# A four-layer graph network on one core: a queue of its own for layer 1's last row chain, and later checks in layer 2's wide pass

## The chip, the cores and the metric

The kernel runs on one core of one Trainium2 chip. The metric is the device time of one execution in microseconds (us). Three runs of the kernel before the change took 1104.93, 1107.02 and 1113.25 us; their median is 1107.02 us.

The engines are called as the profile calls them: PE multiplies matrices (PEld loads its stationary operand), DVE is the vector engine, ACT the scalar engine, POOL is GpSimd, and SP issues the large DMA loads.

## The reference, cut to what matters

`x` has 4096 rows of 64 numbers, `adj` is a 4096 x 4096 matrix of zeros and ones in float32 (64 MB). Four layers follow each other, each of the form `x = layernorm(x + f(x, adj))`:

```
# layer 0: mean over neighbours, a linear map, relu, rows of unit length
deg = sum(adj, 1) + 1
z = concat([x, (adj @ x + x) / deg]) @ W + b ; out = relu(z) / norm
# layer 1: hyperbolic attention, curvature c = 1/r**2
adj_att = sigmoid(left[:, None] + right[None, :] + b) * adj
support = einsum('ij,ijd->id', adj_att, logmap(x_i, x_j))
out = proj(expmap(x, support))
# layer 2: of each row's edges the last 100 count, with weights halving from the end
w = mask * where(pos > 0, 0.5 ** (k - pos), 0) ; out = w @ (x @ weight) + bias
# layer 3: as layer 1, with curvature 1
```

The fast path holds only if every entry of `adj` is 0 or 1. So each loaded piece of `adj` is also checked, once in the whole program: a vector instruction counts the entries that are neither. Any such entry would send the program into a slow path, which is not run here.

## The kernel before, in words

The columns of `adj` are cut into four groups `s` of 1024 output rows, taken as 3, 2, 1, 0 (`GROUPS`). In each layer a group walks over 16 loads `g` = 15 down to 0 (`load`, L698: 1 MB each, one tile `edges`, six buffers), each of two blocks `j` = 2g+1 and 2g of 128 source rows. So `adj` is read four times, 256 loads in all. A buffer is free for the load six later when PE, and the check if there is one, have read it.

Layer 0 has on PE eight matmuls for a load (L1414). Layers 1 and 3 (`attend`) have for each block the logits and squares on PE (L1059 to L1065), a sigmoid and a square on ACT (L1074, L1077), and two instructions on DVE (L1080, L1082), whose result goes back to PE (L1037). Layer 2 has a wide pass over groups 3 and 2 together (`wide_pass`), then a narrow pass for group 1 and one for group 0. In a pass, PE counts edges into a running PSUM tile (`count`, L1569), ACT takes a power of two of it (`weights_of`, L1576), and PE adds up with the rows of `halves` (`add_up`, L1581). The next block's count goes into the same PSUM tile, so PE waits there for ACT's reading. `halves` of group s is made by `supports(s)`, from the group's finished rows of layer 1: ACT casts to `x_hl` (L1252), POOL takes the remainder (L1253), PE transposes (L1258), ACT copies to `x_t` (L1261), PE multiplies (L1268), ACT and DVE write `halves` (L1274, L1275).

Between these stand the row chains: `end_0` after a group of layer 0, `move` after a group of layers 1 and 3, `end_2` after a group of layer 2, each with some hundred small instructions one after the other. They are Python generators in two queues. A call of `tick(1)` (one for each block and one for each pair of blocks in `attend`, four for each load in layer 0, two for each block in the wide pass) lets the head of each queue emit its instructions up to its next `yield n`; then it rests n ticks. Only the head of a queue moves. The wide pass has no ticks in its first five blocks. `need(tag)` ticks until a piece is done: in the wide pass it is asked for group 1 before load g = 7 (`need((2, 1))`) and for group 0 before g = 3 (`need((2, 0))`). What `need` emits stands in the instruction stream with none of the pass's own work between.

`move(1, 1)` is queued (`later(move_s)`, queue 0) when `attend` of group 1 ends, and runs on POOL with a few DVE instructions, beside group 0's attention. `move(1, 0)`, the last, is queued behind it in queue 0 and runs on DVE (its names end in `_1`). `supports(1)` waits in queue 1 for the tag of `move(1, 1)`; `supports(0)` is queued in queue 0 behind `move(1, 0)`. Both `move`s keep their 64 columns `u` and the row sums in one tile `u_1` with one buffer.

Inside `tc.manual_schedule(engines=FIXED)`, which holds layers 0 and 2, PE and ACT execute in the order of the program text; DVE and POOL are put in order by the framework's planner at build time.

`check` (L838, one DVE instruction on 1 MB and a small one that reads its count): layer 0 checks the loads with even g, layer 2 those with odd g, for all groups. Layer 0 writes its unused output into `junk`, layer 2 into the tile `t` of the attention.

Of the kernel before, what the change touches and what calls it, by code (L numbers as in the profile page):

```python
# [10 lines left out]
F32 = mybir.dt.float32  # L11
# [8 lines left out]
P = 128  # L20
N = 4096
D = 64
# [8 lines left out]
NW = N // WW  # L31
WB = WW // P
# [26 lines left out]
def gnn_stack_kernel(  # L59
# [15 lines left out]
    nc = tc.nc  # L75
    V = nc.vector
# [11 lines left out]
    for src, at in ((b0, 0), (b2, D), (b_att1, 2 * D), (b_att3, 2 * D + 1), (r1, 2 * D + 2)):  # L88
        n = src.shape[0]
# [479 lines left out]
    def stream(fits):  # L569

        with ExitStack() as st:

            def pool(name, bufs=1, **kw):
                return st.enter_context(tc.tile_pool(name=name, bufs=bufs, **kw))
# [4 lines left out]
            row = pool("f_row")  # L579
            lefts = pool("f_lefts", 2)  # L580
            aux = pool("f_aux", 1, space=PSUM)
            GROUPS = tuple(reversed(range(NW)))
# [5 lines left out]

            FIXED = {mybir.EngineType.PE, mybir.EngineType.Activation}
            ROW_ENGINES = FIXED | {mybir.EngineType.DVE}  # L590
            queues, place, done, held = ([], []), [0, 0], set(), []

# [32 lines left out]
                    mark(True)  # L627

            def later(steps, second=False, wait=0):
                queues[second].append([steps, place[1] + wait])  # L630

            def in_turn(tag, *parts):
                for part in parts:
                    yield from (part or ())
                done.add(tag)
# [4 lines left out]

            def need(tag):
                while tag not in done:
                    assert queues[0] or queues[1], tag
                    tick(1)

            def soon():
# [49 lines left out]
            def load(s, g):  # L696
                a = loads.tile([P, 2, WW], F32, name="edges")
                nc.sync.dma_start(a, adj[s, :, 2 * g : 2 * g + 2, :])  # L698

                return a, a.rearrange("p b i -> p (b i)").bitcast(BF16)[:, 1::2]  # L700

            def grp(name, bufs=None):
                kw = {"bufs": bufs} if bufs else {}
                return row.tile([P, WB, D], F32, name=name, **kw)

            def nums(name, n=WB):
                return row.tile([P, n], F32, name=name)
# [81 lines left out]
            for h in range(2):  # L789
                of = slice(h * D, (h + 1) * D)  # L790
# [11 lines left out]
            for k in range(3):  # L802
                part = float(np.float16(rest))
# [294 lines left out]
            def move(layer, s, sums, curve):  # L1098
# [8 lines left out]
                last = s == GROUPS[-1]  # L1107
                G = Small(not last, "_1" if last else "")
                E = V if last else nc.gpsimd
                nums = G.nums  # L1110
                k, d, uu = nums("k"), nums("d"), nums("uu")
                w, sq = (grp("y"), grp("xw")) if last else (grp("w_att"), grp("sq"))

                if last and layer == 3:

                    all_u = ys.rearrange("p k f -> p (k f)").bitcast(F32)[:, : WB * (D + 1)]
                    all_u = all_u.rearrange("p (k f) -> p k f", f=D + 1)
                else:
                    all_u = row.tile([P, WB, D + 1], F32, name="u_1")
                u, sum_1 = all_u[:, :, :D], all_u[:, :, D]  # L1120
                for part in range(2):
                    yield from free()
                    t = take(F32, P, 2, 2, D + 1)
                    for i in range(2):
                        cols = slice((2 * part + i) * P, (2 * part + i + 1) * P)
                        nc.tensor.matmul(t[:, i], sums[:, cols], centre, start=True, stop=True)
                    yield near()
                    nc.scalar.copy(  # L1128
                        all_u.rearrange("p (h k) f -> p k h f", h=2)[:, 2 * part : 2 * part + 2], t
                    )  # L1130
                    held.pop()
                    yield near()
                E.tensor_mul(w, xg, u)  # L1133
# [34 lines left out]
                y2, xy, den, p, q = (nums(n) for n in ("y2", "xy", "den", "p", "q"))  # L1168
# [18 lines left out]
                px, qd, w2, t = nums("px"), nums("qd"), nums("w2"), nums("mt")  # L1187
# [11 lines left out]
                n = yield from G.rsqrt(t, "n", 12)  # L1199
# [103 lines left out]
            with ExitStack() as lp:  # L1303
# [94 lines left out]
                with tc.manual_schedule(engines=FIXED):  # L1398
                    for s in GROUPS:
                        sums = [ps.tile([P, W], F32, name="acc") for _ in range(2)]  # L1400
                        counts = [ps.tile([P, W], F32, name="acc") for _ in range(2)]
                        parts = ((first, sums, P), (third, counts, D + 1))
                        for g in reversed(range(NB // 2)):
                            a, edge = load(s, g)
                            if s == GROUPS[0] and 2 * g % WB == WB - 2 and g > WB // 2:
                                parts_of(2 * g // WB - 1)
                            if g % 2 == 0:
                                check(s, g, a, own.tile([P, 2, WW], BF16, name="junk"))
                            for k in (1, 0):
                                j = 2 * g + k  # L1410
                                for lhs, accs, m in parts:
                                    for h in range(2):
                                        at = k * WW + h * W
                                        nc.tensor.matmul(  # L1414
                                            accs[h][:m], lhs[:, j, :], edge[:, at : at + W],
                                            start=j == BLOCKS[0], stop=j == BLOCKS[-1],
                                        )
                            if g == s * WB // 2 + 1:

                                for lhs, accs, m in parts:  # L1420
                                    for h in range(2):
                                        for k in range(SB):
                                            nc.tensor.matmul(
                                                accs[h][:m, k * P : (k + 1) * P],
                                                lhs[:, s * WB + h * SB + k, :], ident_b,
                                                start=False, stop=False,
                                            )
                            if s == GROUPS[0] and g == NB // 2 - 3:
                                curve1, curve3, att1, att3 = constants()
                                nc.scalar.dma_start(w2_sb, w2)  # L1430
                                nc.scalar.dma_start(w2_twice[:D], w2)
                                nc.scalar.dma_start(w2_twice[D:], w2)
                                later(in_turn((0, s), linear(0, s, w0_sb[:D, :], own_part)))
                            tick(4)
                        need((0, s))
                        tops = []
                        for h in range(2):
                            top = sb.tile([P, W], F32, name="top")
                            nc.scalar.copy(top, sums[h])
                            low = sb.tile([D + 1, W], F32, name="low")  # L1440
                            nc.scalar.copy(low, counts[h][: D + 1])
                            tops.append((top, low))
                        later(end_0(s, tops))
                        if s > 0:
                            own_of = linear(0, s - 1, w0_sb[:D, :], own_part)
                            later(in_turn((0, s - 1), own_of))
# [11 lines left out]
            def attention(layer, curve, rates, behind):  # L1458

                need((layer, GROUPS[0]))  # L1460
                for n, s in enumerate(GROUPS):
                    if n:
                        need((layer, s, "left"))
                    anchored[0] = n > 0
                    then = GROUPS[n + 1] if n + 1 < NW else None
                    sums = attend(layer, s, rates[n], then)
                    move_s = in_turn((layer, s, "moved"), move(layer, s, sums, curve))
                    if n:
                        later(
                            in_turn((layer + 1, s + 1), there((layer, s + 1, "moved")), behind(s + 1)),  # L1470
                            True, 9,
                        )
                    later(move_s)
                    if n + 1 == NW:
                        later(in_turn((layer + 1, s), behind(s)))
                anchored[0] = False


# [78 lines left out]

            def load_2(s, g):
                a, edge = load(s, g)
                if g % 2 == 1:  # L1560
                    junk = sb.tile([P, 2, WW], F32, name="t", bufs=3).bitcast(BF16)
                    check(s, g, a, junk[:, 0, :].rearrange("p (b i) -> p b i", b=2))
                return edge
# [64 lines left out]
            t, g = nums("m1", 1), nums("g1", 1)  # L1628
# [26 lines left out]
    with tc.tile_pool(name="fit_ps", bufs=1, space=PSUM) as ps:  # L1655
        t = ps.tile([1, P], F32, name="fit_t")
# [52 lines left out]
```

## Time and profile before

| what | value |
|---|---|
| median of three runs | 1107.02 us |
| profiled execution: span from first to last instruction | 1106.6 us (the profile gives no other time of it) |
| PE, DVE, ACT, POOL busy | 1001.9, 915.5, 803.1, 273.1 us |
| mean granted clock of PE | 0.966 |
| one check (L838) | 2.29 us, 64 of them |
| layer 0, about | 0 to 190 us |
| layer 1, about | 190 to 522 us |
| layer 2: wide pass, two narrow passes, about | 515 to 625, 625 to 761 us |
| layer 3, about | 761 to 1106 us |

The stages are read off the lines of the chain of waits (L1414, L1037, L1569 and L1581, L1037 again). A line of the chain is: start, duration, engine, tile written, source line, number of instructions. A line of a timeline has besides the operation, its operands and, in brackets, the idle time of the engine before it and what ended that.

### The profile page before, as it was taken

The numbers are of one execution on the slowest core, as the hardware profiler recorded it, in microseconds if no ns is written. First come the engines' busy times: TensorE is split into PE (matmuls) and PEld (weight loads), VectorE is DVE, ScalarE is ACT, GpSimd is POOL, SyncE is SP. The second block draws the span as 40 slices with busy tenths as digits, with TensorE's granted clock in tenths as the row PEclk, the third lists the DMA queues.
The fourth block names the chain that finished last, engine by engine and source line by source line (L and its number), as shares of the span: only waits on it lengthen the run. The fifth ranks groups of instructions, "written<-read, shape, count | busy, mean of one in ns | idle before, by whom it ended". The sixth has DMA issues, their size and how long they took to land.

```text
span 1106.6 us, 13832 instructions
## 1 busy us (share of the span) xinstructions
PE 1001.9 (91%) x4949; PEld 392.4 (35%) x4949; DVE 915.5 (83%) x1452; ACT 803.1 (73%) x892; POOL 273.1 (25%) x649
## 2 busy tenths in 40 slices
PE   4998998889999999998998998789899999999980
PEld 2454554333333333332333332223333333333320
DVE  5777977989999999999456484545999999999996
ACT  0003123879999999897676788889899998998960
POOL 0011212010144443525500010000001444346173
PEclk8999999889999999999998999799999999999995
DMA  9999999536565565654877987477545656666400
GB/s 341 378 419 380 370 423 396 190 131 244 191 240 219 188 238 219 228 194 148 333 304 275 362 289 261 155 270 285 203 169 211 251 214 229 228 227 227 164 1 23
DMA packets 38581, 271.63 MB, mean 245 GB/s; under 512 B 4710, under 2 KB 4710, under 8 KB 5734
## 3 DMA queue, kind: packets, MB, share of 16 engines
q1 hardware_dynamic: 37728, 270.03, 64.8%
q8 instruction: 41, 0.67, 0.2%
q10 hardware_dynamic: 774, 0.63, 0.2%
q14 instruction: 38, 0.31, 0.1%
HBM read 269.58 MB, written 1.05 MB: 245 GB/s over the span
## 4 chain that ended last, share of the span: by engine, by line
PE 55%; DVE 24%; ACT 9%; DMA 5%; POOL 3%; issue 2%; ACTq 0%; SPq 0%; POOLq 0%; DVEq 0%
PE acc L1037 15%; PE z L1569 9%; DVE t L1082 7%; PE z L1059 7%; PE z L1065 6%; PE z L1062 6%; DVE t L1080 6%; DMA edges<-in_adj_dram 4%; PE acc L1581 3%; PE acc L1414 3%; ACT sq L1077 3%; ACT sq L1576 2%; DVE junk L838 2%; ACT sig L1074 1%; PE z L1581 1%
## 5 line engine op out<-in xcount | busy, mean ns | idle before, releaser
L1080 DVE SCALAR_TENSOR_TENSOR t<-z,sig 128x1024 f32<-128x1024 f32 x256 | 308.8, 1217 | 13.0 <-ACT sq L1077 6.8
L1077 ACT ACTIVATE sq<-z,turn 128x1024 f32<-128x1024 f32 x256 | 277.8, 1111 | 45.1 <-PE z L1065 18.4
L1082 DVE SCALAR_TENSOR_TENSOR t<-sq,t 128x2048 f32<-128x2048 f32 x128 | 297.3, 2322 | 0.5
L1074 ACT ACTIVATE sig<-left_b,right 128x1024 f32<-128x1024 f32 x256 | 285.9, 1146 | 1.9 <-DVE t L1080 1.3
L1037 PE MATMUL acc<-t,xe 128*64 128x512 f32 x1024 | 255.2, 608 | 17.2 <-DVE t L1082 16.8
L1059 PE MATMUL z<-edges,two_i 128*128 128x512 bf16 x512 | 201.2, 393 | 7.4 <-DVE t L1080 7.4
L1065 PE MATMUL z<-dst,src 74*128 74x512 f16 x512 | 195.5, 382 | 0.0
L1062 PE MATMUL z<-lo_hi,hi_lo 128*128 128x512 f16 x512 | 194.4, 380 | 0.0
L1576 ACT ACTIVATE sq<-z,at_edge 128x512 bf16<-128x512 f32 (+1 forms) x192 | 149.3, 828 | 46.0 <-PE z L1569 43.5
L838 DVE SCALAR_TENSOR_TENSOR t<-edges 128x2048 bf16<-128x2048 f32 x32 | 73.0, 2287 | 54.2 <-DMA edges<-in_adj_dram 54.2
L1037 PEld LDWEIGHTS acc<-t,xe 128*64 128x64 f32 x1024 | 63.8, 136 | 145.6 <-issue 83.8
L1569 PE MATMUL z<-edges,pass_by 128*128 128x512 bf16 x248 | 89.5, 401 | 17.9 <-ACT sq L1576 17.8
L1414 PE MATMUL acc<-edges,first 128*128 128x512 bf16 x256 | 80.1, 394 | 17.6 <-DMA edges<-in_adj_dram 17.3
L1059 PEld LDWEIGHTS <-two_i 128*128 128x128 bf16 x512 | 50.3, 98 | 128.9 <-issue 82.3
L1569 PE MATMUL z<-edges,enter 128*128 128x512 bf16 x256 | 91.0, 398 | 0.0
L1414 PE MATMUL acc<-edges,third 128*65 128x512 bf16 x256 | 80.0, 394 | 0.0
L838 DVE SCALAR_TENSOR_TENSOR junk<-edges 128x2048 bf16<-128x2048 f32 x32 | 73.1, 2286 | 4.7 <-DMA edges<-in_adj_dram 4.4
L1065 PEld LDWEIGHTS <-src 74*128 74x128 f16 x512 | 49.2, 96 | 70.5 <-issue 8.0
L1062 PEld LDWEIGHTS <-hi_lo 128*128 128x128 f16 x512 | 50.4, 98 | 57.1 <-issue 11.7
L1581 PE MATMUL acc<-sq,halves 128*64 128x512 bf16 x384 | 62.5, 403 | 1.0 <-ACT sums L1088 0.8
L869 POOL TENSOR_TENSOR sq<-z 128x512 f32<-128x512 f32 x8 | 14.2, 1776 | 164.3 <-DVE z L868 132.2
L1133 POOL TENSOR_TENSOR w_att<-x,u 128x512 f32<-128x512 f32 x6 | 15.6, 2595 | 141.2 <-ACT u L1128 141.2
(375 smaller groups left out, 940.9 us busy)
## 6 DMA issues: line engine op xcount, KB each, us to landing
edges<-in_adj_dram SPq DMA_DIRECT2D x256, 1024.0 KB, 4.7
x<-in_x_dram SPq DMA_DIRECT2D x4, 256.0 KB
out_dram<-x ACTq DMA_DIRECT2D x2, 256.0 KB
out_dram<-x SPq DMA_DIRECT2D x2, 256.0 KB
w_sb<-in_L_gnn_W_dram ACTq DMA_DIRECT2D x1, 32.0 KB, 4.8
w_twice<-in_L_gnn_weight_dram ACTq DMA_DIRECT2D x2, 16.0 KB, 8.6
given<-in_L_gnn_b_dram ACTq DMA_DIRECT2D x1, 0.2 KB
given<-in_L_gnn_bias_dram ACTq DMA_DIRECT2D x1, 0.2 KB
```

The source lines that it names most:

```text
L838: V.scalar_tensor_tensor(junk, a, 0.0, a, ALU.not_equal, ALU.not_equal, accum_out=odd[:, n : n + 1])
L1037: it = nc.tensor.matmul(acc[h * D : (h + 1) * D, :], xe[:, j, :], t[:, k, h * W : (h + 1) * W], start=j == BLOCKS[0], stop=j == BLOCKS[-1],)
L1059: nc.tensor.matmul(half, two_i, edge[:, at : at + W], start=True, stop=False)
L1062: nc.tensor.matmul(half, hi_lo[:, of], lo_hi[:, to], start=False, stop=False)
L1065: last = nc.tensor.matmul(half, src[:, of], dst[:, to], start=False, stop=True)
L1074: nc.scalar.activation(sig, left_b, AF.Sigmoid, bias=right[:, j : j + 1])
L1077: nc.scalar.activation(sq[:, k], zp, AF.Square, bias=turn, scale=-1.0 / UNIT)
L1080: V.scalar_tensor_tensor(t[:, k], zp, 0.0, sig, ALU.max, ALU.mult)
L1082: V.scalar_tensor_tensor(t, sq, HIGH**2, t, ALU.add, ALU.mult)
L1414: nc.tensor.matmul(accs[h][:m], lhs[:, j, :], edge[:, at : at + W], start=j == BLOCKS[0], stop=j == BLOCKS[-1],)
L1569: nc.tensor.matmul(z[:, h : h + W], lhs, rhs[:, h : h + W], start=j == BLOCKS[0], stop=True, skip_group_check=True,)
L1576: nc.scalar.activation(w, z[:, :n], AF.Exp, bias=at_edge, scale=-LN2)
```

## The change

It has two parts.

First, a third queue. For the last group of layer 1, `move(1, 0)` and `supports(0)` go to queue 2; each tick then steps `move(1, 1)` in queue 0, `supports(1)` in queue 1 and the head of queue 2. The last `move` of layer 1 takes its `u` from the tile `z0` and its row sums from a small tile of their own; the row sums are copied there by DVE (two small copies), and ACT copies 256 columns instead of 260.

Second, which checks are made when. For groups 3 and 2 (those of the wide pass), layer 2 checks g = 0, 1, 2, 3, 5, 7, 9, 11 where it checked 1, 3, ..., 15; layer 0 checks g = 4, 6, 8, 10, 12, 13, 14, 15 where it checked 0, 2, ..., 14. The number of checks stays 64. Groups 1 and 0 stay as they were.

```diff
-            queues, place, done, held = ([], []), [0, 0], set(), []
+            queues, place, done, held = ([], [], []), [0, 0], set(), []
...
             def later(steps, second=False, wait=0):
-                queues[second].append([steps, place[1] + wait])
+                queues[int(second)].append([steps, place[1] + wait])
...
+            def checked_later(s, g):
+
+                return g in (0, 1, 2, 3, 5, 7, 9, 11) if s in GROUPS[:2] else g % 2 == 1
...
                 else:
-                    all_u = row.tile([P, WB, D + 1], F32, name="u_1")
-                u, sum_1 = all_u[:, :, :D], all_u[:, :, D]
+                    all_u = None if last else row.tile([P, WB, D + 1], F32, name="u_1")
+                if all_u is None:
+                    u, sum_1 = grp("z0"), nums("sum_1")
+                else:
+                    u, sum_1 = all_u[:, :, :D], all_u[:, :, D]
...
-                    nc.scalar.copy(
-                        all_u.rearrange("p (h k) f -> p k h f", h=2)[:, 2 * part : 2 * part + 2], t
-                    )
+                    of = slice(2 * part, 2 * part + 2)
+                    if all_u is None:
+                        nc.scalar.copy(
+                            u.rearrange("p (h k) f -> p k h f", h=2)[:, of], t[:, :, :, :D]
+                        )
+                        V.tensor_copy(
+                            sum_1.rearrange("p (h k) -> p k h", h=2)[:, of], t[:, :, :, D]
+                        )
+                    else:
+                        nc.scalar.copy(
+                            all_u.rearrange("p (h k) f -> p k h f", h=2)[:, of], t
+                        )
...
-                            if g % 2 == 0:
+                            if not checked_later(s, g):
                                 check(s, g, a, own.tile([P, 2, WW], BF16, name="junk"))
...
-                    later(move_s)
+                    apart = 2 if n + 1 == NW and layer == 1 else 0
+                    later(move_s, apart)
                     if n + 1 == NW:
-                        later(in_turn((layer + 1, s), behind(s)))
+                        later(in_turn((layer + 1, s), behind(s)), apart)
...
             def load_2(s, g):
                 a, edge = load(s, g)
-                if g % 2 == 1:
+                if checked_later(s, g):
```

More of the change, by code (lines that the diff above doesn't have):

```diff
@@ L642, in need @@
                 while tag not in done:
-                    assert queues[0] or queues[1], tag
+                    assert any(queues), tag
                     tick(1)
```

## The prediction

> **What bounds the kernel now.** I read the page first, for the span and the engines.
>
> ```profile
> span 1106.6 us, 13832 instructions
> PE 1001.9 (91%) x4949; PEld 392.4 (35%) x4949; DVE 915.5 (83%) x1452; ACT 803.1 (73%) x892; POOL 273.1 (25%) x649
> ```
>
> PE is busy 91% of the span, so a gain has to come from the remaining 9%, and from its slow-clock stretches. Second, the chain of waits between 500 and 680 us, where the change acts.
>
> ```profile
> 565.02 2.12 ACT sq L1576 x2
> 567.14 0.51 ACT x_hl L1252
> 567.72 1.17 POOL x_hl L1253
> 568.93 0.64 PE aux L1258 x8
> 569.59 1.02 ACT x_t L1261
> 570.65 0.64 PE z L1268 x16
> ...
> 594.69 0.52 ACT x_hl L1252
> 595.28 1.68 POOL x_hl L1253
> 597.00 0.63 PE aux L1258 x8
> 597.66 1.02 ACT x_t L1261
> 598.73 1.03 PE z L1268 x16
> 599.76 3.41 PE z L1569 x8
> ```
>
> These are two holes in the wide pass. At each, `need` stops the pass until `supports` has run from ACT to POOL to PE to ACT to PE. The first is for group 1, the second for group 0. ACT's timeline sizes them: L1576 starts for a new block every 2.90 us, but at 565.02 and, two blocks later, at 575.13: 10.11 - 5.80 = 4.3 us lost. The second: 592.58 to 605.87, so 13.29 - 5.80 = 7.5 us lost. Together 11.8.
>
> Third, DVE's timeline at the border of layers 1 and 2.
>
> ```profile
> 517.95 2.28 DVE L838 SCALAR_TENSOR_TENSOR t<-edges 128x2048 bf16<-128x2048 f32 x1
> ...
> 520.16 2.28 DVE L1082 SCALAR_TENSOR_TENSOR t<-sq,t 128x2048 f32<-128x2048 f32 x1
> ...
> 529.00 0.16 DVE L754 TENSOR_SCALAR n<-mt 128x8 int32<-128x8 int32 x1
> ```
>
> A check of the wide pass stands ahead of the last product of layer 1, which PE (0.97 us) and ACT (2.15 us) then wait for. Three more follow at 522.36, 524.57 and 526.78, and `move(1, 1)`, ready on POOL at 513.52, gets its L754 only behind them.
>
> Fourth, layer 0, where half of the checks lie: SP's waits, then DVE and PE near the start.
>
> ```profile
> SPq L698 <- DVE junk L838: 101.0, 28, 6.8
> ```
>
> ```profile
> 18.04 2.27 DVE L838 SCALAR_TENSOR_TENSOR junk<-edges 128x2048 bf16<-128x2048 f32 x1
> ...
> 22.57 0.29 DVE L1332 COPY given_b<-aux 128x131 f32<-128x131 f32 x1
> ```
>
> ```profile
> 22.91 1.01 PE L822 MATMUL aux<-one_row,att_row 1*128 1x1 f32 x4 [4.34 <-DVE given_b L1332]
> ```
>
> In layer 0 the loads wait 101.0 us (28 times, 6.8 the longest) for checks to release a buffer, and 37.2 for PE's L1414. The DMA engines are busy 96 to 99% there (windows from 20 to 195 us), so a load issued late is mostly not caught up. At the start PE waits 4.34 us for `given_b`, behind the checks at 18.04 and 20.35.
>
> **The third queue.** I counted ticks from the yields. The pass's first tick is in block 26. In the kernel before, `move(1, 1)` ends in the first tick of `need((2, 1))`, the 23rd. Only then does `move(1, 0)` begin; its first product starts at 566.74, its rows are written at 591.5, 24.8 us later, and by its last rest of 13 ticks it ends in the first tick of `need((2, 0))`. So `supports(0)` is emitted there, all of it.
>
> After, `move(1, 0)` steps from the first tick: its copies in blocks 26 and 25, its tanh in the 11th tick (block 21), the rest in the 12th, its end in the 25th, which lies inside `need((2, 1))`. `supports(1)` keeps its place, ticks 23 to 29. So `supports(0)` starts inside the first hole, ends in the next block, and the second hole is gone: -7.5 us. What takes its place:
> - *The first hole grows.* One `x_hl` buffer serves both groups, and ACT is in order: the second cast (0.55 with its gap) stands ahead of `x_t` of group 1. Then eight transposes (0.64) before PE counts again, and after that count the product of group 0 (0.64, and about 0.1 for its copy). Together +1.9.
> - *Work that lay in the hole.* The eight matmuls with `centre` ran at 566.74 to 567.9 while PE waited. They move into full blocks: +1.2. ACT has 0.78 idle per block: the `u` copies (0.39, 0.38) fit; the square (0.63) and a `halves` cast (0.58) may cost 0.3. DVE's two new copies (0.2 each, by its 128x8 rows) lie in its idle time (16.6 of 40 us busy from 525 to 565); without cover they cost 0.4.
> - *The slow clock.* After the second hole PE ran slow: 1.05 us a pair of matmuls at 599.57, 0.61 at 604.69; L1569 and L1581 take 4.4 us where they take 2.4. PE had idled 2.64 and 1.10 us. In the first hole it idled 1.03 and 1.08 and stayed fast. Without `centre` it idles from 566.8 to 568.9 and then some 1.6, 3.7 us in all, as in the second hole. So a drop may move there: +2.0, or nothing. I take 6 in 10 of it, 1.2.
>
> [...]
>
> Sum: -7.5 + 1.9 + 1.2 + 0.3 + 1.2 = -2.9, between -4.4 (no drop, all on ACT hidden) and +2 (a drop, and ACT waiting 4 us once for DVE). Queued behind such waits: tanh holds all later L1576, hence PE. By rows, DVE needs from the last copy to the tanh 1.1 + 1.3 + 4.1 = 6.5 us (568.35 to 576.68, less a `halves` product and a wait), and seven ticks of half a block leave 10.1; a check in front takes 2.29. The rest takes 10 us, 14.6 with two checks (576.82 to 591.44), and has five blocks, 14.5, up to the hole. POOL's side of `move(1, 1)` gets DVE's L754 some 9 us earlier and is not late.
>
> **The checks in layer 2.** g = 15 and 13, four checks, leave the border. The last L1082 can start at 518.03 instead of 520.16. PE still counts until 521.5, so PE gains about 1.0 and ACT up to 2.1: -1.5, between -1.0 and -2.1. The four checks come back at g = 2 and 0, where DVE is busy 7.6 of 25 us (600 to 625) and PE, not DVE, releases the buffers (SP waits 217.9 us for L1569 there and later, 5.6 for these checks). I cost them at nothing; without that cover they are 4 x 2.29 = 9.2.
>
> **The checks in layer 0.** Two places get two more, and each group's last two go, where they delay no load that starves.
> - *Group 3, from 0 us.* The check of g = 15 can run before 17.66, as DVE idles 6.40 us there behind a small DMA; that of g = 13 likely lands before `given_b`: +2.3 on PE's first wait, and on the tenth load (30.20), as DMA has drained by 32.7. If DVE's order puts two checks into the idle stretch, nothing; if it puts four behind 17.66, +4.6. It can also free a place (-2.3). I take +1.0.
> - *Group 2, from 55 us.* g = 15 lands at 54.9, in DVE's 3.87 us wait for PE: free. g = 13 falls into `end_0`'s chain, which has 1.16 us idle there: +1.1 to +2.3 on the check at 80.96, which releases the loads at 83.23, 89.76 and 93.12. I take +1.7.
>
> Sum for layer 0: +2.7, from -2.3 to +6.9. From there everything is serial, so shifts add: -2.9 - 1.5 + 2.7 = -1.7. Against the profiled execution that is 1106.6 - 1.7 = 1104.9. The median of the runs stands 0.4 above the span, so **1105.3**.
>
> **Rivals.**
> - *Layer 0 eats it all (slower).* Checks at g = 13 to 15 hold buffers while DVE works on constants and rows: +6.9 instead of +2.7, 1109.5. For it: 101.0 us of waiting on checks. Against it: DVE's idle 6.40 and 3.87 us. It decides from +4.4 on.
> - *The rows come too early (slower).* Ahead of the tanh or of `x(0)` in the hole DVE runs two checks (4.6), ACT stands, PE stands behind it, and the clock drops: 4.6 + 4.6 less slack, about +9, 1114. For it: no slack on PE per block. Against it: the counted 10.1 and 14.5 us.
> - *More goes than one hole (faster).* At 689.12, 696.87 and 701.91 ACT takes three early sigmoids of layer 3 in the narrow pass, each with two table loads: 1.28 + 1.15 + 1.28 = 3.7, 11.1 in all. The order that is planned anew may leave some out. With two out, layer 0 at nothing and no clock drop: 1105.3 - 7.4 - 2.7 - 1.2 = 1094. Against it: nothing in the diff touches them.
> - *Nothing moves.* If `move(1, 0)` ends later than the hole, the stop moves behind it: 1107.
>
> **How the numbers follow.** Forecast 0.50 (its own range 1101 to 1110), layer 0 0.18, early rows 0.12, more than one hole 0.12, nothing moves 0.08. About 1% (11 us) is what a measurement of this kernel can tell from no change: the runs spread over 8 us. Below 1096: most of the third rival, 0.11, the rest of it lying just above. Above 1118: half of the second and a tail of the first with the 6 us that the slowest run stands above the median, 0.11. Within 1%: 0.78. The range 1094 to 1116 takes in -2.1 - 4.4 - 2.3 with one early sigmoid gone (1107.0 - 8.8 - 3.7 = 1094.5) and the second rival with 2 us on top.
>
> **What would show it.** Right: no `need` stop near 590, L1576 at 2.90 us through there, first hole about 2 us longer or slow afterwards, the last L1082 of layer 1 without a check ahead of it, layer 0 ending 1 to 5 us later with more waiting on L838. Wrong: tanh (L1164) waiting over 1 us, PE waiting for `x_hl` over 5 us, a changed number of table loads, or layer 0 as early as before.

## The result, and the profile after

The changed kernel takes 1107.76 us (median of 14 runs, 1105.63 to 1114.76); the kernel before, run beside it on the same chip, takes 1107.74 us (14 runs, 1102.04 to 1115.95). The ratio is 1.0001, 95% interval 0.9984 to 1.0019: no difference to within 0.2%, where the prediction had 1105.3 us.

The profiled execution of the changed kernel took 1114.76 us and is the slowest of its 14. In it PE also ran slow (granted clock 0.50) from 671.8 to 678.6 and from 729.8 to 736.7 us, where the blocks of the narrow passes took some 4 us longer than before; in the profile before, a slow stretch begins at 672.6 us, but is only 3.4 us long, and from 710.2 to 765 us the granted clock is 1.00. So below, places are compared and not spans. First the page.

```profile
span 1113.0 us, 13744 instructions
PE 1004.0 (90%) x4862; PEld 394.4 (35%) x4949; DVE 915.9 (82%) x1454; ACT 804.6 (72%) x892; POOL 272.8 (25%) x649
```

Busy times are those of before within 2.1 us on each engine. Nothing was saved or added in work, so whatever changed is in waits and in the clock. The lines answer to those of before with numbers higher by 4 (early in the file) to 17 (L1569 is now L1586, L1576 is L1593).

**The wide pass.** ACT's timeline of the changed kernel where the first hole was (start, duration, instruction, and in brackets ACT's idle time ahead of it and what ended that):

```profile
563.31 2.12 ACT L1593 ACTIVATE sq<-z,at_edge 128x1024 bf16<-128x1024 f32 x2 [0.78 <-PE z L1586]
565.32 0.62 ACT L1268 CAST x_hl<-x 128x512 f16<-128x512 f32 x1
568.85 0.62 ACT L1268 CAST x_hl<-x 128x512 f16<-128x512 f32 x1 [2.91 <-POOL x_hl L1269]
...
574.07 1.11 ACT L1593 ACTIVATE sq<-z,at_edge 128x1024 bf16<-128x1024 f32 x1 [0.64 <-PE z L1586]
```

From 563.31 to 574.07 is one block, which takes 10.8 us, where 2.90 is the usual. The reader sees both groups in it: the second cast to `x_hl` is group 0's, and it stands ahead of `x_t` of group 1 and waits 2.91 us until POOL has read the one buffer. PE's timeline in the same place:

```profile
568.15 0.62 PE L1274 MATMUL aux<-ident,x_hl 128*128 128x128 f16 x8 [3.05 <-POOL x_hl L1269]
570.43 1.03 PE L1284 MATMUL z<-w_hl,x_t 128*128 128x64 f16 x16 [1.67 <-ACT x_t L1277]
```

PE idles 3.05 and 1.67 us, with 0.62 us of transposes between, and after that the 16 products take 1.03 us where before they took 0.64: the slow clock, granted 0.50 from 569.4 to 576.2 us. The longer first wait is not the clock but POOL, whose remainder for `x_hl` began while DVE ran a check:

```profile
564.79 2.29 DVE L842 SCALAR_TENSOR_TENSOR t<-edges 128x2048 bf16<-128x2048 f32 x1
566.01 2.08 POOL L1269 TENSOR_TENSOR x_hl<-x,x_hl 128x512 f16<-128x512 f32 x1 [33.89 <-ACT x_hl L1268]
```

It took 2.08 us there, and 1.16 in the kernel before (at 567.72) as well as 1.15 for group 0 (at 569.54), where no check was running when it began. So the transposes start 0.9 us later after the block's power of two than before.

This table gives for each block the time from the first L1593 (L1576 before) of the block ahead of it to its own, in us. Blocks that are not named took the same within 0.4 us, but for three in the two slow stretches named above.

```
                       before   after
wide, 30                4.27     2.32     border of layers 1 and 2
wide, 25, 24, 22        2.90 each   3.34, 3.34, 3.00   copies of move(1, 0)
wide, 15, 14            7.22, 2.90  10.75, 4.45        first hole
wide, 7, 6              8.99, 4.30  2.90, 2.90         second hole
narrow, group 1, 19     3.49     5.86
narrow, group 1, 17, 16 1.69, 1.56  2.85, 1.92
```

The second hole is gone (-7.5), the first has grown (+5.1), and the pass ends at 621.24 us where it ended at 625.36. The last two rows give 3.9 of these 4.1 us back, in a place where the prediction had nothing.

**The border.** DVE's timeline at the last product of layer 1:

```profile
517.20 2.29 DVE L1086 SCALAR_TENSOR_TENSOR t<-sq,t 128x2048 f32<-128x2048 f32 x1
524.85 0.17 DVE L758 TENSOR_SCALAR n<-w 128x8 int32<-128x8 int32 x1 [5.36 <-POOL w L1225]
```

The product starts at 517.20, behind L758 alone, and the next thing that DVE does is L758 for `move(1, 1)`, after 5.36 us of idle time. No check stands there any more, ahead of the product or behind it.

**Layer 0.** SP's waits, DVE's checks at the start, and PE's first wait:

```profile
SPq L698 <- DVE junk L842: 101.0, 28, 6.7
```

```profile
8.14 2.28 DVE L842 SCALAR_TENSOR_TENSOR junk<-edges 128x2048 bf16<-128x2048 f32 x1
...
18.31 2.28 DVE L842 SCALAR_TENSOR_TENSOR junk<-edges 128x2048 bf16<-128x2048 f32 x1
...
20.52 0.29 DVE L1348 COPY given_b<-aux 128x131 f32<-128x131 f32 x1
```

```profile
20.86 1.01 PE L826 MATMUL aux<-one_row,att_row 1*128 1x1 f32 x4 [3.84 <-DVE given_b L1348]
```

Four checks stand ahead of `given_b`, and it still comes 2.05 us earlier than before (22.57): the small `w_hl` instructions, which had kept DVE waiting until 17.66 us, now come behind the third check. The tenth load goes out at 27.54 us instead of 30.20, SP waits for checks as long as before, and layer 0 ends at 180.84 us instead of 181.34.

**The narrow pass of group 1.** While its first half runs, the two groups of the wide pass go through `end_2` and their row chains, on DVE. Before:

```profile
625.21 2.29 DVE L838 SCALAR_TENSOR_TENSOR t<-edges 128x2048 bf16<-128x2048 f32 x1 [4.16 <-DMA edges<-in_adj_dram]
```

In this line DVE, which had been idle, waits for the load, and the chain begins behind it, at 629.67 us (L1494). Two more checks stand in the chain itself, between the first `z` and `y`, the rows that ACT needs next:

```profile
634.56 2.28 DVE L838 SCALAR_TENSOR_TENSOR t<-edges 128x2048 bf16<-128x2048 f32 x1
...
642.22 2.28 DVE L838 SCALAR_TENSOR_TENSOR t<-edges 128x2048 bf16<-128x2048 f32 x1
```

After the change the chain begins at 625.54, and three checks stand in it:

```profile
625.88 0.42 DVE L1515 SCALAR_TENSOR_TENSOR z<-aux,given_b 128x256 f32<-128x256 f32 x1
626.21 2.28 DVE L842 SCALAR_TENSOR_TENSOR t<-edges 128x2048 bf16<-128x2048 f32 x1
...
628.42 0.69 DVE L1521 TENSOR_TENSOR z<-z,x 128x512 f32<-128x512 f32 x1
...
632.52 2.28 DVE L842 SCALAR_TENSOR_TENSOR t<-edges 128x2048 bf16<-128x2048 f32 x1
...
640.18 2.29 DVE L842 SCALAR_TENSOR_TENSOR t<-edges 128x2048 bf16<-128x2048 f32 x1
...
643.35 1.54 DVE L900 TENSOR_TENSOR y<-x,ym 128x512 f32<-128x512 f32 x1
```

One check more (by its order that of group 1's g = 13), which used to run while DVE had nothing to do, now stands inside the chain, between L1515 and L1521. From the first `z` to `y` is 15.7 us before and 17.8 after. What waits for `y` is in ACT's timeline, before and after, and what follows in PE's, after:

```profile
646.95 0.62 ACT L899 CAST ys<-y 128x512 f16<-128x512 f32 x1 [0.66 <-DVE y L896]
```

```profile
644.92 0.62 ACT L903 CAST ys<-y 128x512 f16<-128x512 f32 x1 [3.02 <-DVE y L900]
```

```profile
647.22 0.39 PE L1586 MATMUL z<-edges,pass_by 128*128 128x512 bf16 x1 [4.11 <-ACT sq L1593]
...
648.66 1.06 PE L1598 MATMUL acc<-sq,halves 128*64 128x512 bf16 x4
```

The casts of `y` have their place in ACT's order, ahead of the next power of two; ACT stands 3.02 us (0.66 before), PE 4.11 (1.74 before), and then PE runs slow (granted 0.50 from 647.9 to 651.3 us): 1.06 us for four matmuls that take 0.62.

### The profile page after: what moved, and what is told of

It is laid out like the page before. It is cut to its first block, busy times and chain, and to the rows that moved or that the text cites. A ratio compares the mean times of both kernels' runs of the same rounds, so it can differ in the third digit from the quotient of the medians.

```text
span 1113.0 us, 13744 instructions
## 1 busy us (share of the span) xinstructions
PE 1004.0 (90%) x4862; PEld 394.4 (35%) x4949; DVE 915.9 (82%) x1454; ACT 804.6 (72%) x892; POOL 272.8 (25%) x649
## 5 line engine op out<-in xcount | busy, mean ns | idle before, releaser
L1086 DVE SCALAR_TENSOR_TENSOR t<-sq,t 128x2048 f32<-128x2048 f32 x128 | 297.5, 2324 | 0.5
L1041 PE MATMUL acc<-t,xe 128*64 128x512 f32 x1024 | 258.4, 614 | 16.8 <-DVE t L1086 16.1
L1063 PE MATMUL z<-edges,two_i 128*128 128x512 bf16 x463 | 182.2, 394 | 6.8 <-DVE t L1084 6.8
L1593 ACT ACTIVATE sq<-z,at_edge 128x512 bf16<-128x512 f32 (+1 forms) x192 | 150.6, 829 | 48.0 <-PE z L1586 44.9
L1586 PE MATMUL z<-edges,pass_by 128*128 128x512 bf16 x241 | 90.3, 411 | 21.4 <-ACT sq L1593 20.7
L1430 PE MATMUL acc<-edges,first 128*128 128x512 bf16 x241 | 77.1, 396 | 17.5 <-DMA edges<-in_adj_dram 16.9
L1586 PE MATMUL z<-edges,enter 128*128 128x512 bf16 x240 | 87.6, 408 | 0.4
```

The lines of the kernel that those rows point to most:

```text
L1041: it = nc.tensor.matmul(acc[h * D : (h + 1) * D, :], xe[:, j, :], t[:, k, h * W : (h + 1) * W], start=j == BLOCKS[0], stop=j == BLOCKS[-1],)
L1063: nc.tensor.matmul(half, two_i, edge[:, at : at + W], start=True, stop=False)
L1086: V.scalar_tensor_tensor(t, sq, HIGH**2, t, ALU.add, ALU.mult)
L1430: nc.tensor.matmul(accs[h][:m], lhs[:, j, :], edge[:, at : at + W], start=j == BLOCKS[0], stop=j == BLOCKS[-1],)
L1586: nc.tensor.matmul(z[:, h : h + W], lhs, rhs[:, h : h + W], start=j == BLOCKS[0], stop=True, skip_group_check=True,)
L1593: nc.scalar.activation(w, z[:, :n], AF.Exp, bias=at_edge, scale=-LN2)
```

## The experiments

My theory after the two profiles: the change saves what the prediction had, in layer 2's wide pass and at its border, and a check that the planner now lays into DVE's row chain gives the saving back. The rivals: that one of the two parts alone moves the time (the queue for nothing, the checks for a loss in layer 0), or that the slow clock in the first hole takes it all. Where an expectation fell, the text behind it says so. All ratios are to the kernel before, in runs on the same chip.

### The queue alone

```diff
             def checked_later(s, g):
-                return g in (0, 1, 2, 3, 5, 7, 9, 11) if s in GROUPS[:2] else g % 2 == 1
+                return g % 2 == 1
```

> The third queue with u in z0, and the checks as they were before (odd g in layer 2 for all groups). Theory A (the second hole goes, the first grows and often takes the slow clock along; the four border checks still cost 2 us): no stop for group 0 near 590, first hole about 9 us over two blocks, end of the wide pass 1 to 3 us earlier than before, whole 1105 to 1108. Theory B (what the wide pass gains is only lost to the chance of slow clock stretches): end of the wide pass the same 1 to 3 us earlier and the whole 1104 to 1106. If the gain of the change came from the checks alone, this kernel would end its wide pass as before.

Measured: 1110.98 us, ratio 1.0011 (0.999 to 1.0031); the time is above the range of theory A, but the kernel before took 1109.59 us beside it on that chip. Border as before (4.47 us for block 30), no second hole, blocks 15 and 14 take 10.52 and 3.36; and in the narrow pass block 19 takes 5.86 us, 17 and 16 take 2.81 and 2.57. DVE's timeline there has the check in the same place, ahead of L1521, though no check was moved in this kernel:

```profile
633.83 2.28 DVE L842 SCALAR_TENSOR_TENSOR t<-edges 128x2048 bf16<-128x2048 f32 x1
...
636.03 0.69 DVE L1521 TENSOR_TENSOR z<-z,x 128x512 f32<-128x512 f32 x1
```

So the queue takes the second hole away and is worth nothing, and the third check in the chain comes with the queue: DVE's order is planned anew for the whole program.

### The checks alone

The third queue and the tile `z0` are taken out again, on both sides; `checked_later` stays.

```diff
-            queues, place, done, held = ([], [], []), [0, 0], set(), []
+            queues, place, done, held = ([], []), [0, 0], set(), []
...
-                    later(move_s, apart)
+                    later(move_s)
```

> The new list of checks alone, rows in the two old queues. My prediction's step for layer 0 says +2.7 us there; the changed kernel's profile says -0.5. Theory A: layer 0 ends within 1 us of before, last L1082 product of layer 1 about 2 us earlier, both holes as before (4.3 and 7.5 us), and the narrow pass gives the 2 us back, since the check of group 1's g = 15 now stands in the row chain of end_2: whole 1106 to 1109. Theory B: the 2 us stay to the end, 1104 to 1106. Rival C (front checks cost in layer 0): layer 0 ends 2 us or more later, whole 1109.

Measured: 1104.66 us, ratio 0.9959 (0.9939 to 0.9978): 4 to 5 us faster. The border's block takes 2.38 us, both holes stand (8.19 and 3.52; 8.90 and 3.92), and block 19 of the narrow pass takes 3.50 us, as before, with two checks in the chain. That fells theory A's thought that the new list of checks by itself loads the row chain. The border explains 1.9 us of the gain; where the rest lies, a single profile (of an execution of 1107.11 us, one of the slowest here) does not show.

The first hole took 1.6 us more here than before, although its text is the same: PE idled the same 1.03 and 1.10 us, and in this execution a slow stretch of 3.4 us followed, from 568.7 us; before, none did (granted 1.00 from 560 to 590 us).

### `supports(1)` without its rest of nine ticks

POOL had written the last rows of group 1 (L1234, 530.95 and 1.18 long) at 532.1 us. Its next line in the changed kernel's timeline is the remainder at 566.01 shown above, with 33.89 us of idle time ahead of it. So the hole is no wait for rows; it is where the program text puts the work.

```diff
-                yield pool_done(15, 3) if G.on_pool else after(72)
+                if G.on_pool:
+                    yield 1 if layer == 1 and s == GROUPS[2] else pool_done(15, 3)
+                else:
+                    yield after(72)
```

> The changed kernel, but the chain of group 1 ends its rest after its last addition at the next tick instead of nine ticks later, so that supports of group 1 is emitted three to four blocks ahead of the point where it is needed. In the changed kernel POOL has written these rows at 532.1 us and idles 33.9 us until the cast. Theory A: the first hole (9.4 us over blocks 15 and 14 in the profile) goes too, its work of about 2.6 us on PE moves into full blocks, end of the wide pass 5 to 7 us earlier than in the changed kernel, whole 1099 to 1103. If the hole were made by late rows and not by the rest of nine ticks, nothing moves: 1107. If what the wide pass gains is always given back in the narrow passes, the wide pass ends early and the whole stays at 1105 to 1107.

Measured: 1102.79 us, ratio 0.996 (0.9938 to 0.9983). ACT's timeline has the pieces of `supports` spread between powers of two; the cast of group 0, say, and what follows it without a wait:

```profile
571.69 0.61 ACT L1271 CAST x_hl<-x 128x512 f16<-128x512 f32 x1
572.20 1.12 ACT L1596 ACTIVATE sq<-z,at_edge 128x1024 bf16<-128x1024 f32 x1
```

The first hole's loss falls from 9.4 us to some 3.4 in five blocks (17, 16, 15, 12, 11: 3.62, 3.65, 3.35, 3.63, 3.65), and the pass ends at 614.84 us. Block 19 of the narrow pass still takes 5.86, with three checks in the chain. The two are separate.

### All eight later checks last

For the groups of the wide pass, layer 2 checks g = 0 to 7 and layer 0 checks g = 8 to 15.

```diff
-                return g in (0, 1, 2, 3, 5, 7, 9, 11) if s in GROUPS[:2] else g % 2 == 1
+                return g < 8 if s in GROUPS[:2] else g % 2 == 1
```

> The changed kernel with the checks of groups 3 and 2 pushed all the way: layer 0 checks g = 8 to 15, layer 2 checks g = 0 to 7. If checks at the front of a group cost in layer 0 (my prediction, about +1.1 to 2.3 us for each one in the row chain), layer 0 ends 2 to 6 us later than before; if DVE has room for them there, as the changed kernel's -0.5 says, within 1 us. The border keeps its 2 us, the row chain of group 0 in the wide pass is free of checks. Whole 1105 to 1109 without a price in layer 0, 1109 to 1113 with it.

Measured: 1111.33 us, ratio 1.0019 (0.9998 to 1.004). That is the range with a price in layer 0, but the interval reaches down to no difference. In the first 36 us of layer 0 stand eight checks where the change has six, the tenth load goes out at 30.92 us (27.54 in the change), and layer 0 ends at 185.42 us. In other profiles of kernels whose layer 0 was not touched it ended at up to 186.41 us, so its end settles nothing; the start shows that the tenth load's gain with the change's list is lost with this one. The intervals of this kernel and of the change overlap.

### One check of group 1 at another place

The check that stood in the chain (group 1, g = 13) is made in layer 0, that of g = 0 in layer 2. All else of the text is the change; DVE's order is planned anew.

```diff
             def checked_later(s, g):
+                if s == GROUPS[2]:
+                    return g in (0, 1, 3, 5, 7, 9, 11, 15)
                 return g in (0, 1, 2, 3, 5, 7, 9, 11) if s in GROUPS[:2] else g % 2 == 1
```

> The changed kernel, but of group 1 layer 2 checks g = 0 in place of g = 13 (layer 0 takes 13 in place of 0). In every profile with the third queue so far, block 19 of the narrow pass of group 1 starts 5.86 us after block 20 and block 17 another 2.8 later; without the queue 3.49 and 1.69. In the changed kernel DVE does this check at 626.2, inside the row chain of end_2 (between L1515 and L1521), before the change at 625.2, ahead of the chain. Theory A (the queue's gain is given back by that check in the chain, and by the slow clock that the longer wait brings): block 19 at 3.4 to 3.8 us, block 17 at 1.7, whole 3 to 4 us below the changed kernel, 1103 to 1105. Theory D (the wait at block 19 is made by something else that comes early, such as ACT's or POOL's part of the chain): block 19 stays at 5.9, whole 1107 to 1109.

Measured: 1101.93 us, ratio 0.9945 (0.9919 to 0.9972), better than theory A had it. DVE's chain, with no check between `z` and the next steps and one later, then ACT at the same place:

```profile
624.88 0.41 DVE L1517 SCALAR_TENSOR_TENSOR z<-aux,given_b 128x256 f32<-128x256 f32 x1
625.32 0.69 DVE L1523 TENSOR_TENSOR z<-z,x 128x512 f32<-128x512 f32 x1
...
632.44 2.29 DVE L844 SCALAR_TENSOR_TENSOR t<-edges 128x2048 bf16<-128x2048 f32 x1
...
637.95 0.68 DVE L902 TENSOR_TENSOR y<-x,ym 128x512 f32<-128x512 f32 x1
```

```profile
640.77 0.62 ACT L905 CAST ys<-y 128x512 f16<-128x512 f32 x1
```

From the first `z` (624.53) to `y` 13.4 us, and ACT does not wait for `y` at all. Blocks 19 to 16 take 2.70, 1.46, 1.69 and 1.56 us: 7.4 in all, against 12.1 in the changed kernel and 8.2 before.

The run took out more than the one check: another, which the change has at 640.18, now stands behind `y` (at 639.30). So it has one check ahead of `y` where the change has three. The other runs fill in the steps; the last experiment below leaves none there, and in all of them the chain begins 3.1 us after the pass's first power of two:

```
checks ahead of y   first z to y   ACT waits for y   blocks 19 to 16   runs
0                   10.8           0                 7.4               all three mends
1                   13.4           0                 7.4               this one
2                   15.7           0.7               8.2               before; checks alone
3                   17.8           3.0               11.9 to 13.1      the change; queue alone; the four others
```

Each check makes the chain some 2.1 to 2.6 us longer. One costs the pass nothing, the second 0.8 us, the third 3.8 to 4.9, of which the block that waits takes 2.4 and the blocks behind it the rest. In the profile of the change, with the third check, a slow stretch of PE begins 0.7 us behind the end of that wait (granted 0.50 from 647.9 to 651.3 us); in that of the kernel before there is none at this place (granted 1.00 from 604.4 to 672.6 us). So what the change would be worth without the third check alone was not measured; this run, without two of them, can only be an upper estimate, and comes to about as much as the checks alone.

### The sigmoids of layer 3 behind the last power of two

ACT's timeline in group 0's narrow pass, the changed kernel; an exponential ends just ahead of these lines and the next starts at 693.76:

```profile
690.00 1.28 ACT L1078 ACT_TABLE_LOAD   x1
691.30 1.15 ACT L1078 ACTIVATE sig<-left_b,right 128x1024 f32<-128x1024 f32 x1
692.47 1.28 ACT L1593 ACT_TABLE_LOAD   x1
```

```diff
-                        nc.scalar.activation(
+                        it = nc.scalar.activation(
...
+                        if layer == 3 and s == GROUPS[0]:
+                            in_order(it.ins, last_exp[0].ins)
```

> The changed kernel with layer 3's first sigmoids held behind the last power of two of layer 2, so that ACT's three early ones (with two table loads each, near 690 to 706) cannot stand in the narrow pass of group 0. My prediction priced them at 3.7 us each as a chance for a larger gain. If they cost what their rows say: blocks 30, 28 and 27 of that pass at 1.6 to 2.0 instead of 5.05 us, three sigmoids of 1.15 us more at the start of layer 3, whole 6 to 8 us below the changed kernel. If ACT's time there is hidden behind the row chain of end_2, the pass ends as before: within 2 us.

Measured: 1100.59 us, ratio 0.9936 (0.9914 to 0.9959). The three blocks of group 0 that held a sigmoid take 1.45, 1.45 and 1.69 us instead of 5.05, 5.04 and 5.04. The price of 3.7 that the prediction's third rival had for each holds within 0.4 us; the diff left all three in, as the prediction had it. The whole gains 7.3 us, less than these blocks, since the three sigmoids now stand at the start of layer 3.

### Filling the first hole

32 transposes ahead of those of group 1, and 32 small products ahead of its own, go to PE. Their output is overwritten; what the kernel computes is unchanged.

```diff
+                if s == GROUPS[2]:
+                    for n in range(4 * WB):
+                        k = n % WB
+                        nc.tensor.transpose(t[:, k * P : (k + 1) * P], ident16, ident16)
...
+                if s == GROUPS[2]:
+                    for n in range(4 * WB):
+                        nc.tensor.matmul(
+                            t[:, n % WB, :], ident16, w2_hl[:, 0], start=True, stop=True
+                        )
```

> The changed kernel with idle work for PE in the first hole: 32 transposes of the identity ahead of the transposes of group 1's rows, 32 small products ahead of its product; both are overwritten by the real ones, the result is the same. If the slow clock after the hole comes from PE's idling (3.05 and 1.67 us in the changed kernel), no slow stretch follows, and blocks 15 and 14 start 10.75 and 4.45 us apart no more but about 10 and 2.9. If it comes otherwise, the slow stretch stays and the filler costs up to 1 us.

A single execution took 1111.23 us; layer 0 ended at 186.33 us in it, 5.5 us later than in the changed kernel with the same text of layer 0, so that time says nothing of the hole. The place itself, PE's timeline:

```profile
569.38 1.96 PE L1276 MATMUL aux<-ident 128*128 128x128 f16 x32
...
573.86 0.64 PE L1293 MATMUL z<-w_hl,x_t 128*128 128x64 f16 x16 [0.73 <-ACT x_t L1281]
```

Ahead of the last line stand, besides, the eight transposes of `x_hl` and 32 fillers of 1.10 us. The 16 products take 0.64 us, not 1.03, and PE idled no longer than 0.73 us at a time. POOL's remainder differs as well: it began just ahead of a check (570.39) and not behind one.

```profile
570.36 1.16 POOL L1269 TENSOR_TENSOR x_hl<-x,x_hl 128x512 f16<-128x512 f32 x1 [33.68 <-ACT x_hl L1268]
```

The same stretch in the windows view (time, then busy us and instructions of PE, PEld, DVE, ACT, POOL, then the granted clock, the DMA share and GB/s), first with the filling, then the change:

```profile
560.00:580.00 20.00, 18.54 (x189) 9.46 (x186) 13.72 (x47) 13.69 (x16) 2.86 (x2) 1.00 0.68 266
```

```profile
560.00:580.00 20.00, 15.06 (x109) 7.12 (x108) 9.54 (x15) 12.07 (x14) 3.23 (x2) 0.83 0.61 226
```

The granted clock is 1.00 where it was 0.83, and blocks 15 and 14 take 8.70 and 3.73 us instead of 10.75 and 4.45: 2.8 us less, with more work on PE. Not all of it is the clock: up to the transposes at 571.57 the two differ by 0.9 us, which is POOL's remainder (1.16 against 2.08); from the transposes to block 14 it is 8.5 us against 10.4. So of the hole's growth of 5.1 us, 1.9 are the slow clock, 0.9 POOL's remainder behind a check, and 2.3 the longer chain. That the filling kept the clock up rests on one execution, set beside the one profile of the change. Block 19, not filled, took 5.87 us.

How much idle time brings the slow clock the rows do not settle. With 4.11 us of idle time in one piece, up to 647.22 us, came a slow stretch of 3.4 us; with the 3.05 and 1.67 us of the changed kernel's first hole, and 0.62 us of transposes between, one of 6.8. The second hole before had 2.64 and 1.10 us, with 0.63 us of transposes between, and a slow stretch of 6.8 us (granted 0.50 from 597.5 to 604.4 us); the first hole's 1.03 and 1.10 us were followed by a slow stretch with the checks alone and by none before.

### All three mends together

`supports(1)` without its rest, the sigmoids behind the last power of two, and for group 1 the checks g = 0 to 6 and 15 in layer 2.

```diff
+                if s == GROUPS[2]:
+                    return g in (0, 1, 2, 3, 4, 5, 6, 15)
```

> The changed kernel with the early supports of group 1 (third run of the first set), layer 3's sigmoids held back, and group 1's checks in layer 2 at g = 0 to 6 and 15, which leaves the row chains of the narrow pass free of checks. If the three gains add (4 to 6, 6 to 8 and 3 to 6 us): 1090 to 1096. If they hit one common wait, the row chain of end_2, not below 1098.

Measured: 1094.33 us, ratio 0.9866 (0.9828 to 0.9904, 6 runs). It beats both kernels, and the product of the three ratios, 0.984, lies in the interval. Layer 2 ends 19.2 us before that of the kernel before, of which layer 3 gives back 3.5 in its first group, where the sigmoids now stand. No check is left ahead of `y`, block 19 takes 2.71 us, and the three blocks of the sigmoids 1.45, 1.46 and 1.68. Block 12 of the wide pass takes 5.66 us, 2.0 more than in the run with the early `supports` alone: POOL's remainder for group 0 began at 572.99, behind a check at 572.87, and took 3.18 us instead of 1.16, and PE waited 2.14 us for it.

## Why the prediction was right, and where its steps were not

The time came out 2.5 us above the forecast, but so near by luck: two errors cancelled, layer 0 and the pass behind the wide one. By its steps, in us:

| step | predicted | measured | from |
|---|---|---|---|
| second hole | -7.5 | -7.5 | blocks 7 and 6 |
| first hole's chain | +1.9 | +2.3 | with the hole filled, blocks 15 and 14 |
| POOL's remainder behind a check | 0 | +0.9 | start of the transposes |
| the slow clock moves | +1.2 (0 or 2.0) | +1.9 | with and without the filling |
| `centre` and ACT's extras in full blocks | +1.5 | +0.9 | blocks 25 to 22 |
| border | -1.5 | -1.8 | blocks 30 and 29 |
| layer 0 | +2.7 | -0.5 | its end, 181.34 to 180.84 |
| layer 1 up to its border | 0 | -0.4 | the start of the wide pass |
| four checks at g = 2 and 0 | 0 | 0 | blocks 5 to 0 at 2.90 |
| end of the wide pass | -1.7 | -4.1 | 625.36 to 621.24 |
| narrow pass of group 1 | 0 | +3.9 | blocks 19 to 16 |

- *The holes and the border: right.* The pieces ran in the order that the count of ticks gave, and the second cast waited for the one buffer, as written. The clock's drop came, and at 1.9 us near the 2.0 that the text had for one (1.2 was 2.0 times its chance). But the ground for it, that the first hole had idled 1.03 and 1.08 us (1.10 in the trace) and stayed fast, was one execution: with the checks alone the same hole, with the same pieces of idle time, was slow for 3.4 us. The sum left POOL's remainder at its 1.17 us; behind a check it took 2.08, a term that it did not have. The tanh, which was to wait over 1 us if the rows came too early, did not wait.
- *Layer 0: wrong.* "I take +1.0" for group 3 assumed that DVE's order keeps its wait for `w_hl` and gets another check behind it. It does hold four checks ahead of `given_b`, but the first of them at 8.14 us and the wait for `w_hl` gone, so PE's wait ended 2.05 us earlier. The bound of -2.3 that the text had was nearer for the start. For group 2, +1.7 was forecast, and its stretch from one row sum to the next grew from 42.1 to 42.8 us, +0.7. Layer 0 as early as before was named in the text as what would show this step wrong. One profile's end would be little to go by; but of the five profiles with this text of layer 0, the four without a slow stretch between 33 us and its end (the change: granted 1.00 from 26.7 to 181 us) have it end at 180.84 to 182.04 us, against 181.34 before, so +2.7 is out.
- *"From there everything is serial, so shifts add": wrong.* The sum took the -4.1 at the end of the wide pass to arrive at the end of the program. DVE's order behind it is no fixed order that merely shifts; it was planned anew for a changed program, and one check of a group that the change leaves alone went from DVE's idle time into the chain that ACT waits for, as a third where two stood: +3.9 us. The prediction asked what would be late next inside the wide pass only.
- *The rivals.* Layer 0 did not eat it, the rows did not come too early, the move did end inside the hole, and no sigmoid went away. What came was none of the four.

The two parts alone, 1.0011 for the queue and 0.9959 for the checks, multiply to 0.9970; measured is 1.0001 with an interval from 0.9984. The intervals of the parts reach far enough to allow it, but their middles do not meet. I have no run that says whether the checks lose something beside the queue, or whether this is the spread of the profiles' slow stretches. Also open is why the planner sets that check where it does: the runs show that it comes with the queue and goes with the swap, not the cost in the plan that decides it.

## What to carry to other kernels

Where a planner orders an engine, a change in one stage is a new order in all of them; look at what the chain that follows gets laid into it, above all at long instructions without a deadline, like checks: here the first in the chain cost nothing, the second 0.8 us and the third about 4, so the slack has to be counted and not assumed. A wait that is removed from the instruction stream is worth its length only if PE's other waits do not grow: here the 7.5 us were paid back as 5.1 in the first hole, 1.9 of it the clock and 0.9 POOL behind a check, and 3.9 in the next pass. And ask of each hole whether data or the text sets it: POOL's 33.89 us of idle time ahead of `x_hl` said that an earlier place was free to take, and that was worth more than the queue.

## What the runs showed of the hardware

- With idle time of PE in two pieces (3.05 and 1.67 us) came the slow clock (0.83 granted over 20 us, 0.50 from 569.4 to 576.2); with 64 small instructions in these gaps, 3.06 us of work, it stayed at 1.00, in one execution, and the stretch behind the gaps was 1.9 us shorter for more work.
- In the profiles before and after, where POOL's remainder for `x_hl` (128x512) overlapped a check or a product (L1082; L1086 after) on DVE, the one that began second took longer. The two remainders that began during a check (at 595.28 before and 566.01 after) took 1.67 and 2.08 us and ended 1.02 and 1.01 us behind that check's end; the other six took 1.15 to 1.17. The four products that began during a remainder took 2.71 to 2.72 us, where their mean is 2.32, and ended 2.14 to 2.15 us behind the remainder's end.
- A switch of ACT's table took 1.28 us, and around the three early sigmoids the next instruction started 0.01 us behind it; a sigmoid set between two powers of two cost 3.6 us of its block (5.05 against 1.45).
- Slow stretches of PE (granted clock 0.50) of 3.4, 6.8 and 10.2 us stand in the profiles before and after, partly at other places: that from 597.5 to 604.4 us only before, those from 569.4 to 576.2 and from 729.8 to 736.7 us only after. Layer 0 ended at 180.84 us in the profile of the change and at 186.33 us in that with the filled hole, whose layer 0 has the same text. A single profile says nothing on a few us at the end of a stage; the places do.
